# A re-tuned order for a planned macaron kernel, with a third of its last additions on two other engines

## The chip, the cores and the metric

The kernel runs on one core of a Trainium2 chip. The metric is the device time of one launch in microseconds (us), as the median over runs. The engines are named as the profile names them: PE (TensorE matmuls), DVE (VectorE), ACT (ScalarE), POOL (GpSimd) and SP (SyncE, which issues DMAs).

## The reference

The input `x` has 2 sequences of 2048 tokens with 256 features, so 4096 tokens. Three blocks follow each other, each with a residual and a layer norm in front:

```python
x = x + 0.5 * ffn(layernorm(x), gate_up, down, router)
x = x + attn(layernorm(x), conv_w, conv_b, wq, ..., proj_w, proj_b)
x = x + 0.5 * ffn(layernorm(x), gate_up, down, router)
```

`ffn` is a mixture of 8 experts of width 176. Each token goes to the 2 experts with the largest router logits, weighted by a softmax over those two; an expert computes `(silu(h @ gate) * (h @ up)) @ down`. `attn` is a causal convolution of 3 taps to queries, keys and values of width 64, then causal softmax attention with 8 heads inside blocks of 128 tokens, then two output projections. All is float32.

## The kernel before, in words

**Tiles.** The tokens lie in 8 groups of 512, each held in SBUF as `X[g]` with 4 tiles of 128 tokens. Groups 0 to 3 are one sequence, 4 to 7 the other. Each half (the first and the second `ffn`) handles the groups in two chunks: groups 0 to 2 and 3 to 7 in the first half, 0 to 4 and 5 to 7 in the second.

**A half.** For each group, `logits` normalizes the tokens, writes them to a DRAM table `hd` and computes the router logits. For each chunk, `route` (mostly small DVE steps with one-hot rows `oh` and `ot`, and PE sums `psl`) sorts the chosen tokens by expert into slots of 128 rows. `expert` then takes the slots in pairs. POOL gathers the rows of a slot from `hd` by an indirect DMA (L1113), PE transposes them into `ptr` (L1124), and DVE or ACT copies them to `hsT`. PE multiplies by gate and up into `pgu` (L1165), ACT takes a tanh (L1179), DVE finishes the gating (L1185 to L1188). PE transposes the result into `pm` (L1195), it is copied to `hmT`, PE multiplies by down into `po` (L1218, L1224), and two copies put it in `ys`. In the first half SP writes `ys` to a DRAM table `yd`. In the second half POOL scatters each slot to a table `y` (L1240). Each pair needs the register values that say which expert's weights it takes; `address` loads them for up to four slots in a row at once, for PE and for SP.

**Between the halves.** `combine` gathers the two results of each token with POOL (L1329) and adds them with DVE (L1339). `attention` normalizes again (`h_a`, L543 on DVE or L548 on ACT), runs the convolution, and then loops over 4 blocks of 128 tokens per group: scores `ps` (L1633), mask and maximum on DVE (L1642, L1651), exponentials on ACT (L1667), a product with the reciprocal of the sum on POOL (L1678), transposes `pst` (L1688), context `pcx` (L1705) and the projection with its residual (L1735).

**The end.** `gather_all` loads, for two tiles at a time, the two results of each token from `y` with SP into one of four `s` buffers (L1283, 512 KB). Four DVE additions (L1304) weight them and add them to `X[g]`, and SP stores two tiles (L1314). The loads of groups 5 to 7 need every scatter of the last chunk.

**The order of the work.** Nothing is issued in program order. Each piece is a `step` with a cost per engine that could do it, and `Plan.emit` lists the steps: the one that can start first goes next, and among those that can start at the same time, the one with the greatest priority. A step's priority is the longest chain of costs behind it plus a bias, `plan.bias`, which the table `RANK` sets for each group, chunk or stage. A step with two engines prefers the first one named and takes the other when the first is not free within 0.3 us:

```python
main = next(iter(s.costs))
if e != main and free[main] < t + 0.3:
    continue
if pick is None or t < at - 0.02 or s.prio > pick.prio:
    at, pick = t, s
```

The order found is written out and held on every engine, DMA queues of SP and POOL included. So each engine's queue is fixed, and an instruction that waits holds up all behind it on that engine. Buffers come from pools of fixed size (`SLOTS`), and a step waits for a free one.

Of the kernel before, what the change touches and what calls it, by code (L numbers as in the profile page):

```python
# [10 lines left out]
AF = mybir.ActivationFunctionType  # L11
ALU = mybir.AluOpType
# [9 lines left out]
NS = TB // P  # L22
# [35 lines left out]


RANK = {  # L60
    "logits1": (2852, 2216, 3314, 3481, 1963, 1827, 1743, 3136),
    "route1": (2091, 3734),
    "expert1": (1442, 1598),
    "fold": -360,
    "combine1": (18, 283, -268, 352, -138, -584, -694, -436),
    "attention": (31, 66, 458, -108, 359, -125, -210, -806),
    "logits2": (342, -30, -17, 461, -107, 728, -336, -232),
    "route2": (-70, 1682),
    "expert2": (-795, -757),
    "combine2": (-359, -989),  # L70
    "slope1": (168, 1),
    "slope2": (10, 184),
}


# [22 lines left out]
class Plan:  # L98
# [10 lines left out]
    def step(self, costs, fn, reads=(), writes=(), lat=None, room=(), kb=0):  # L109

        s = Step()
        s.costs, s.fn, s.lat, s.bias, s.start = costs, fn, lat, self.bias, None
        s.kb, s.land = kb, None
        deps, bufs = {}, []
        for wr, accs in ((False, reads), (True, writes)):
            for a in accs:
                b, key = a if isinstance(a, tuple) else (a, None)
                for o, k, w in b.log:  # L120
                    if (w or wr) and (k is None or key is None or k == key) and o is not s:
                        deps[id(o)] = o
                b.log.append((s, key, wr))
                if b not in bufs:
                    bufs.append(b)
                    b.left += 1
        s.used = len(bufs)
        for b in room:
            bufs.append(b)
            b.left += 1  # L130
        s.deps, s.bufs, s.outs = list(deps.values()), bufs, []
        for o in s.deps:
            o.outs.append(s)
        self.steps.append(s)
        return s
# [111 lines left out]
def kernel(  # L247
# [16 lines left out]
    nc = tc.nc  # L264
# [7 lines left out]
    plan = Plan(tc, SLOTS)  # L272
    step, buf = plan.step, plan.buf
# [12 lines left out]
    def work(tag, shape, name, dt=F32):  # L286
        return buf(pools[tag], tag, shape, name, dt)
# [26 lines left out]
    X = [fixed([P, NS, D], f"x_{g}") for g in range(NG)]  # L314
# [159 lines left out]
    for i in range(2):  # L474
        step(
            {"POOL": 0.4},
            lambda e, i=i: nc.gpsimd.iota(
                codes.t[:, i * NG * NH : (i + 1) * NG * NH], pattern=[[P, NG * NH]],
                base=(i - 1) * TOK0 + i, channel_multiplier=1,
                allow_small_or_imprecise_dtypes=True,  # L480
            ),
            writes=[(codes, i)],
# [607 lines left out]
    def expert(k, i0, n):  # L1090
        nm = f"{k.nm}_{i0}"

        beside = k.half == 2 and k.first

        def copied(act, dve):
            return {"ACT": act, "DVE": dve} if beside else {"DVE": dve, "ACT": act}
# [2 lines left out]
        for i in range(i0, i0 + n):  # L1099
# [6 lines left out]
            else:  # L1106
# [6 lines left out]
                lambda e, i=i, hs_=hs_: nc.gpsimd.indirect_dma_start(  # L1113
                    out=hs_(), out_offset=None, in_=k.h.t[:, :],
                    in_offset=bass.IndirectOffsetOnAxis(ap=k.idx.t[:, i : i + 1], axis=0),
                ),
                reads=[k.idx, k.h], writes=[(hs, m)], lat=LAND + 0.5, kb=128,
# [21 lines left out]
        for j in range(n):  # L1139
            get = step(  # L1140
                {"SP": 0.7},
                lambda e, j=j: nc.sync.dma_start(
                    wd.t[j * HALF : j * HALF + TAIL, :],
                    w_down[bass.ds(address(k, i0 + j, 1), TAIL), :],
                ),
                reads=[k.ew], writes=[(wd, j)], lat=LAND, kb=48,
# [13 lines left out]
        def gate_up(e):  # L1160
# [12 lines left out]
            reads=[hsT, k.ew] + [(wx, ("gu", c, j)) for c in range(KD) for j in range(2)],  # L1173
            writes=pgu, room=[hm],
# [5 lines left out]
            reads=[pgu[0]], writes=[hm],  # L1180
# [51 lines left out]
        for j in range(n):  # L1232
            step(
                copied(0.29, 0.34), lambda e, j=j: copy(e, ys.t[:, j, :], po[j].t),
                reads=[po[j]], writes=[(ys, j)],
# [19 lines left out]
        for to, m in [(k.y, i0)] + (  # L1255
# [8 lines left out]
                reads=[ys], writes=[(to, m + j) for j in range(n)], lat=LAND, kb=128 * n,  # L1264
# [6 lines left out]
    def gather_all(g):  # L1271

        k = chunk_of(g, 2)
        want = [(k, i) for i in range(k.NSL)]
        if k.first:
            want += [(k.next, i) for i in range(NLEFT)]
        for t in range(0, NS, 2):
            n = (g - k.g0) * NS + t
            yg = work("s", [P, 2, 2, D], f"y2_{g}_{t}")

            def get(e, t=t, yg=yg):
                r0 = 2 * (g * TB + t * P)
                ins = nc.sync.dma_start(  # L1283
                    yg.t, Y2.t[r0 : r0 + 4 * P, :].rearrange("(t p j) d -> p t j d", p=P, j=2)
                )
                apart(ins, [m for w, m in Y2.puts.items() if w not in want])
                for w in want:
                    tc.add_manual_dep(
                        ins.ins, Y2.puts[w],
                        mybir.DependencyInfo(  # L1290
                            mybir.DependencyClass.Sync, mybir.DependencyReason.DATA
                        ),
                        reason="its rows",
                    )
                Y2.gets.append(ins.ins.name)

            step(
                {"SP": 0.5}, get, reads=[(Y2, w) for w in want], writes=[yg], lat=LAND, kb=512
            )
            for i in range(2):  # L1300
                for j in range(2):
                    step(
                        {"DVE": 0.43},
                        lambda e, i=i, j=j, n=n, t=t, yg=yg: nc.vector.scalar_tensor_tensor(  # L1304
                            X[g].t[:, t + i, :], yg.t[:, i, j, :],
                            k.wt.t[:, j, n + i : n + i + 1], X[g].t[:, t + i, :],
                            ALU.mult, ALU.add,
                        ),
                        reads=[yg, k.wt], writes=[(X[g], t + i)],
                    )  # L1310
            r0 = g * TB + t * P
            step(
                {"SP": 0.35},
                lambda e, r0=r0, t=t: nc.sync.dma_start(  # L1314
                    out[r0 : r0 + 2 * P, :].rearrange("(t p) d -> p t d", p=P),
                    X[g].t[:, t : t + 2, :],
                ),
                reads=[(X[g], t), (X[g], t + 1)], lat=LAND, kb=256,
            )
# [154 lines left out]
    def attention(g):  # L1474
# [4 lines left out]
        if g % GPS == 0:  # L1479
            step(  # L1480
                {"DVE": 0.1}, lambda e: nc.vector.memset(hT.t[:, :, 0:2], 0.0),
                reads=[rstd], writes=[(hT, "pre")],
            )
        else:
# [4 lines left out]
                reads=[(lh, NH - 1), rstd], writes=[(hT, "pre")],  # L1489
# [3 lines left out]
        for i in range(NH):  # L1493
            step(
                {"POOL": 1.3},
                lambda e, i=i: nc.gpsimd.tensor_tensor(
                    X[g].t[:, 2 * i : 2 * i + 2, :], X[g].t[:, 2 * i : 2 * i + 2, :],
                    pb.t.to_broadcast([P, 2, D]), ALU.add,
                ),
                reads=[pb], writes=[(X[g], 2 * i), (X[g], 2 * i + 1)],  # L1500
# [10 lines left out]
        for n0 in (0, 3):  # L1511
# [12 lines left out]
            reads=[pqk, bias], writes=[qk],  # L1524
        )

        for i in range(2):
            step(
                {"SP": 0.52},
                lambda e, i=i: nc.sync.dma_start(kq.t[half2[i], :], qk.t[half2[1 - i], :]),  # L1530
                reads=[qk], writes=[(kq, i)], lat=LAND,
            )

        def conv_v(e):
# [13 lines left out]
            reads=[pv, bias], writes=[vb],  # L1548
        )
        vm = work("vm", [P, NS, HEADS * W], f"vm_{nm}")  # L1550
        for b0 in range(NS // 2):
# [10 lines left out]
            for i in range(2):  # L1562
                b = b0 + i * (NS // 2)
                step(
                    {"ACT": 0.49, "DVE": 0.59},
                    lambda e, b=b, p=pvm[i]: copy(e, vm.t[:, b, :], p.t),
                    reads=[pvm[i]], writes=[(vm, b)],
# [5 lines left out]
        def mmc(e):  # L1573
# [18 lines left out]
            reads=[lc, ident], writes=[pct],  # L1592
# [7 lines left out]
            reads=[pct, cb], writes=[cq],  # L1600
# [19 lines left out]
                )  # L1620

        oT = work("oT", [P, NS // 2, P], f"oT_{nm}")
        for b in range(NS):
            bs = slice(b * P, (b + 1) * P)

            s = work("s", [P, HEADS, P], f"s_{nm}_{b}")
# [113 lines left out]
    for c in range(2):  # L1740
        k = chunks[1, c]
        for g in range(k.g0, k.g1):
            plan.bias = RANK["logits1"][g]
            logits(g, 1)
            if c == 0 and g == k.g1 - 1:
                loads_then(k.rows)
        plan.bias = RANK["route1"][c]
        route(k)
        for i in range(0, k.NSL, 2):
            plan.bias = RANK["expert1"][c] - 0.1 * RANK["slope1"][c] * i  # L1750
            expert(k, i, min(2, k.NSL - i))
            if c == 0 and i == 0:
                step({"PE": 0.1}, ones_once, reads=[(k.y, 0), ones16], writes=[warm])
                plan.bias = RANK["expert1"][c] + 500.0
                hand_on(k)
                loads_last(k)
# [9 lines left out]
    for c in range(2):  # L1766
        k = chunks[2, c]
        plan.bias = RANK["route2"][c]
        route(k)
        for i in range(0, k.NSL, 2):  # L1770
            plan.bias = RANK["expert2"][c] - 0.1 * RANK["slope2"][c] * i
            expert(k, i, min(2, k.NSL - i))
            if c == 0 and i == 0:
                hand_on(k)
# [66 lines left out]
```

## Time and profile before

| what | value |
|---|---|
| median of 3 runs | 714.97 us (713.4 to 716.16) |
| the profiled execution | 717.35 us, of which the span of the profile is 715.6 |
| mean granted TensorE clock | 0.946 |
| PE busy | 650.9 us (91%) |
| DVE busy | 512.4 us (72%) |
| POOL busy | 398.6 us (56%) |
| ACT busy | 317.6 us (44%) |
| DMA | 92.59 MB, 129 GB/s on average |

All durations come from one profiled execution, which took 2.4 us more than the median. Busy time is an average over stages with different limits, so a stage is read on its own: which engine is full in it, and which wait ends last. A row of an operation gives the shortest, the median and the longest of its durations in ns. The time of one instruction contains what it waited for a shared resource after its start, so a maximum far above the median is a wait, not work.

### The profile page before, as it was taken

How to read it: one execution, taken by the hardware profiler on the slowest of the kernel's cores; microseconds unless marked ns; L12 is line 12 of the kernel's file. 1: busy time of each engine (PE TensorE's matmuls, PEld its weight loads, DVE VectorE, ACT ScalarE, POOL GpSimd, SP SyncE). 2: the span in 40 equal slices, each digit the busy share in tenths (PEclk: the TensorE clock that was granted, in tenths of full speed). 3: DMA queues.
4: the chain of work that ended last, by engine and by line, in shares of the span. 5: the costliest groups of instructions: out<-in, count | busy, mean ns of one | idle time of the engine just before them, and what ended most of it. 6: DMA issues, size and time to landing. Idle time of an engine off the chain costs nothing.

```text
span 715.6 us, 14981 instructions
## 1 busy us (share of the span) xinstructions
PE 650.9 (91%) x4837; PEld 492.9 (69%) x4837; DVE 512.4 (72%) x1408; ACT 317.6 (44%) x1008; POOL 398.6 (56%) x458
## 2 busy tenths in 40 slices
PE   6888989999999999799989997979999799999960
PEld 4647868888888754657566564657888687888840
DVE  5884984455448959998999789999845933447735
ACT  4224322222222437495997857448944233223220
POOL 4037207643337877787744622158867477777650
PEclk9699989999999999899999998979999899999995
DMA  9916616564456343023100110027224234439937
GB/s 295 305 63 188 225 49 181 181 181 142 131 139 177 123 119 88 24 59 105 38 32 30 29 47 15 17 80 231 86 87 140 65 118 131 126 110 322 323 109 264
DMA packets 64891, 92.59 MB, mean 129 GB/s; under 512 B 10128, under 2 KB 50352, under 8 KB 64720
## 3 DMA queue, kind: packets, MB, share of 16 engines
q1 hardware_dynamic: 51520, 55.31, 24.1%
q0 software_dynamic: 13296, 36.32, 17.3%
q8 instruction: 41, 0.67, 0.4%
q14 instruction: 34, 0.28, 0.1%
HBM read 56.47 MB, written 37.22 MB: 131 GB/s over the span
## 4 chain that ended last, share of the span: by engine, by line
PE 54%; DVE 33%; issue 4%; POOL 4%; DMA 4%; ACT 1%; SPq 0%; POOLq 0%; DVEq 0%; ACTq 0%
PE pgu_f L1165 20%; PE po_f L1218 8%; PE po_f L1224 5%; DVE nmx_a L1651 4%; DVE s_a L1642 4%; PE ptr_f L1124 3%; DVE x L1339 2%; PE pm_f L1195 2%; DVE oh_f L977 2%; PE pst_a L1688 2%; PE pcx_a L1705 2%; DVE stats_f L505 2%; PE pt_f L564 2%; POOL yg_f L1329 1%; DVE ot_f L985 1%
## 5 line engine op out<-in xcount | busy, mean ns | idle before, releaser
L1113 POOL DMA_INDIRECT hs_f<-hd_f,idx_f x142 | 137.1, 965 | 129.0 <-PE ptr_f L1124 40.6
L1165 PE MATMUL pgu_f<-wx,hsT_f 128*128 x1136 | 184.0, 318 | 1.8 <-DVE hsT_f L299 0.8
L1165 PEld LDWEIGHTS pgu_f<-wx,hsT_f 128*128 128x128 f32 x1136 | 172.7, 193 | 7.5 <-issue 2.6
L1667 ACT ACTIVATE s_a<-s_a,nmx_a 128x128 f32<-128x128 f32 x256 | 98.9, 392 | 11.8 <-DVE nmx_a L1653 11.2
L1678 POOL TENSOR_TENSOR s_a<-s_a,sm_a 128x512 f32<-128x512 f32 x64 | 67.0, 1069 | 61.4 <-DVE sm_a L1674 59.7
L1240 POOL DMA_INDIRECT y<-ys_f,dst_f x71 | 71.0, 1000 | 33.5 <-ACT ys_f L295 13.9
L295 ACT COPY ys_f<-po_f 128x256 f32<-128x256 f32 x123 | 40.8, 375 | 109.8 <-PE po_f L1224 92.4
L1179 ACT ACTIVATE hm_f<-pgu_f 128x352 f32<-128x352 f32 (+1 forms) x72 | 33.0, 460 | 108.8 <-PE pgu_f L1165 106.5
L1218 PE MATMUL po_f<-wx,hmT_f 128*128 x284 | 76.6, 392 | 0.7 <-DVE hmT_f L299 0.7
L1185 DVE SCALAR_TENSOR_TENSOR hm_f<-hm_f,pgu_f 128x352 f32<-128x352 f32 (+1 forms) x72 | 36.7, 510 | 56.2 <-ACT hm_f L1179 55.9
L1329 POOL DMA_INDIRECT yg_f<-yd_f,posi_f x64 | 61.7, 964 | 24.9 <-issue 15.3
L1218 PEld LDWEIGHTS po_f<-wx,hmT_f 128*128 128x128 f32 x284 | 49.5, 192 | 10.6 <-DVE hm_f L1188 3.3
L299 DVE COPY hmT_f<-pm_f 128x384 f32<-128x384 f32 x40 | 22.2, 556 | 44.1 <-PE pm_f L1196 43.9
L1224 PE MATMUL po_f<-wd_f,hmT_f 48*128 48x256 f32 x284 | 51.1, 432 | 0.0
L1339 DVE SCALAR_TENSOR_TENSOR x<-yg_f,wt_f,x 128x256 f32<-128x256 f32 x64 | 41.6, 674 | 11.0 <-DMA yg_f<-yd_f,posi_f 11.0
L1667 ACT ACTIVATION_READ_ACCUMULATOR s_a<-s_a,nmx_a 128x1 f32 x256 | 49.0, 192 | 0.0
L1515 PE MATMUL pqk_a<-haT_a,cw 128*128 128x512 f32 x96 | 46.3, 630 | 0.5 <-ACT haT_a L295 0.5
L1124 PE MATMUL ptr_f<-ident,hs_f 128*128 128x128 f32 x284 | 42.2, 276 | 2.4 <-DMA hs_f<-hd_f,idx_f 2.4
L1688 PE MATMUL pst_a<-ident,s_a 128*128 128x128 f32 x256 | 37.1, 287 | 4.5 <-DVE vm_a L299 2.9
L1642 DVE TENSOR_TENSOR s_a<-ps_a,later 128x512 f32<-128x512 f32 x64 | 40.5, 678 | 0.0
L1688 PEld LDWEIGHTS pst_a<-ident,s_a 128*128 128x128 f32 x256 | 29.2, 146 | 16.3 <-issue 9.5
L1651 DVE TENSOR_REDUCE nmx_a<-s_a 128x8 f32<-128x1024 f32 x32 | 38.7, 1210 | 0.2
(235 smaller groups left out, 1228.0 us busy)
## 6 DMA issues: line engine op xcount, KB each, us to landing
yd_f<-ys_f SPq DMA_DIRECT2D x42, 256.0 KB, 3.6
hd_f<-h_f SPq DMA_DIRECT2D x32, 256.0 KB, 3.2
y<-y SPq DMA_DIRECT2D x16, 512.0 KB, 5.3
wd_f<-in_w_down SPq DMA_DIRECT2D x142, 48.0 KB, 2.7
x<-in_x SPq DMA_DIRECT2D x16, 256.0 KB, 7.0
out<-x SPq DMA_DIRECT2D x16, 256.0 KB, 3.2
hd_f<-hd_f SPq DMA_DIRECT2D x1, 2560.0 KB
hs_f<-hd_f,idx_f POOLq DMA_INDIRECT x142
```

The lines of the kernel that those rows point to most:

```text
L1113: lambda e, i=i, hs_=hs_: nc.gpsimd.indirect_dma_start(out=hs_(), out_offset=None, in_=k.h.t[:, :], in_offset=bass.IndirectOffsetOnAxis(ap ...
L1124: nc.tensor.transpose(pt.t[:, d, j, :], hs_()[:, d * P : (d + 1) * P], ident.t)
L1165: nc.tensor.matmul(pgu[f].t[:, j, :], hsT.t[:, d, j, :], wx.t[:, bass.ds(at + d * GU + f * H, H)], start=(d == 0), stop=(d == KD - 1),)
L1218: nc.tensor.matmul(po[j].t, hmT.t[:, j, :], wx.t[:, bass.ds(at + KD * GU, D)], start=True, stop=False,)
L1224: nc.tensor.matmul(po[j].t, hmT.t[r, n, :], wd.t[r, :], start=False, stop=True)
L1240: ins = nc.gpsimd.indirect_dma_start(out=Y2.t[:, :], out_offset=bass.IndirectOffsetOnAxis(ap=k.dst.t[:, i : i + 1], axis=0), in_=ys.t[:, j ...
L1329: lambda e, j=j, n=n, yg=yg: nc.gpsimd.indirect_dma_start(out=yg.t, out_offset=None, in_=k.y.t[:, :], in_offset=bass.IndirectOffsetOnAxis( ...
L1642: lambda e, h=hd[i], s=s, p=ps[i]: nc.vector.tensor_tensor(s.t[:, h, :], p.t, later.t.to_broadcast([P, NPAIR, P]), ALU.add,),
L1651: nc.vector.tensor_reduce(nmx.t, s.t, AX.X, ALU.max)
L1667: nc.scalar.activation(s.t[:, n, :], s.t[:, n, :], AF.Exp, bias=nmx.t[:, n : n + 1], accum_out=sm.t[:, c : c + 1],)
L1678: lambda e, s=s, sm=sm, h=hd[i]: nc.gpsimd.tensor_tensor(s.t[:, h, :], s.t[:, h, :], sm.t.unsqueeze(2).to_broadcast([P, NPAIR, P]), ALU.mu ...
L1688: nc.tensor.transpose(pt.t[:, c, :], s.t[:, i * NPAIR + c, :], ident.t)
```

## The change

Four things change.

1. The table `RANK` has new values throughout, and new entries: a bias for each pair of slots in each of the four expert stages (`pairs10`, `pairs11`, `pairs20`, `pairs21`, by half and chunk) and one for each of the 32 blocks of attention (`blocks`).
2. In the first chunk of both halves the copies of `expert` name ACT first. Before, that held for the first chunk of the second half only.
3. In `gather_all`, every third tile of the last chunk (4 of the 12 tiles in groups 5 to 7) is scaled in place by ACT and added by POOL; the other tiles keep DVE's additions. A DVE addition now depends on its own tile's part of the loaded buffer.
4. The planner's cost of a last addition on DVE is 0.41 instead of 0.43.

```diff
 RANK = {
-    "attention": (31, 66, 458, -108, 359, -125, -210, -806),
+    "attention": (432, 467, 901, -42, 551, -142, -313, -806),
...
+    "pairs10": (-72, 245, 231, -387, -412, -403, -649, 1, -735),
+    "pairs11": (0, 6, 6, 4, -114, -114, -113, -117, -116, -115, ...),
+    "pairs20": (0, -1, 0, 5, 23, -9, 3, 1, -3, -7, -4, 0, -1, 1, 3, -2, 0),
+    "pairs21": (39, 317, -36, 78, -166, -81, -144, -416, -215, ...),
+    "blocks": (4, 4, 5, 4, 4, 4, 4, 4, 4, 4, ..., 54, -26, -8),
 }
...
-        beside = k.half == 2 and k.first
+        beside = k.first
...
             for i in range(2):
+                if not k.first and (NS * (g - k.g0) + t + i) % 3 == 2:
+
+                    def scaled(e, i=i, n=n, yg=yg):
+                        for j in range(2):
+                            nc.scalar.activation(
+                                yg.t[:, i, j, :], yg.t[:, i, j, :], AF.Copy,
+                                scale=k.wt.t[:, j, n + i : n + i + 1],
+                            )
+
+                    step({"ACT": 0.62}, scaled, reads=[k.wt], writes=[(yg, i)])
+
+                    def added(e, i=i, t=t, yg=yg):
+                        for j in range(2):
+                            nc.gpsimd.tensor_tensor(
+                                X[g].t[:, t + i, :], X[g].t[:, t + i, :], yg.t[:, i, j, :],
+                                ALU.add,
+                            )
+
+                    step({"POOL": 1.1}, added, reads=[(yg, i)], writes=[(X[g], t + i)])
+                    continue
                 for j in range(2):
                     step(
-                        {"DVE": 0.43},
+                        {"DVE": 0.41},
...
-                        reads=[yg, k.wt], writes=[(X[g], t + i)],
+                        reads=[(yg, i), k.wt], writes=[(X[g], t + i)],
...
+        bias0 = plan.bias
         for b in range(NS):
+            plan.bias = bias0 + RANK["blocks"][NS * g + b]
...
-            plan.bias = RANK["expert1"][c] - 0.1 * RANK["slope1"][c] * i
+            plan.bias = (
+                RANK["expert1"][c] - 0.1 * RANK["slope1"][c] * i
+                + RANK["pairs1" + str(c)][i // 2]
+            )
```

The same addition is made to the bias of the second half's pairs.

## The prediction

> **What bounds the kernel now.** I read the page first (engine totals, the 40 slices), then busy time by stretch, then the chain and the timeline of the end, and last the rows of the operations that the change moves. Busy time of each engine in seven stretches (columns: stretch, its length, then PE, PE weight loads, DVE, ACT, POOL, granted clock, DMA share, GB/s):
>
> ```profile
> 62.00:100.00 38.00, 34.48 (x230) 29.29 (x229) 31.46 (x99) 12.55 (x30) 10.84 (x13) 0.87 0.51 159
> 100.00:235.00 135.00, 134.70 (x877) 114.36 (x875) 74.55 (x172) 33.47 (x88) 68.04 (x73) 1.00 0.53 153
> 235.00:300.00 65.00, 60.19 (x392) 35.94 (x388) 56.53 (x127) 30.94 (x100) 51.19 (x55) 0.95 0.32 94
> 300.00:400.00 100.00, 94.54 (x857) 63.19 (x853) 96.85 (x248) 79.84 (x304) 61.19 (x68) 0.98 0.17 49
> 400.00:472.00 72.00, 63.50 (x572) 41.30 (x571) 61.96 (x182) 42.41 (x151) 24.73 (x29) 0.92 0.10 27
> 472.00:693.00 221.00, 214.63 (x1512) 177.75 (x1512) 137.99 (x376) 96.58 (x292) 157.67 (x166) 0.97 0.48 154
> 693.00:716.00 23.00, 0.00 (x0) 0.00 (x0) 10.01 (x25) 0.36 (x1) 2.75 (x3) 0.57 0.65 228
> ```
>
> Four regimes follow. From 100 to 235 (experts of the first half) PE is busy 134.7 of 135.0: nothing but less PE work helps there. From 300 to 400 (attention) DVE has 96.85 of 100 and PE 94.54, so DVE work added or removed there counts nearly in full. From 472 to 693 (experts of the second half) PE is the bound again, with 6.4 us idle. After 693 PE has nothing left, and 23 us are the last scatters, loads, additions and stores. This is the timeline of that end (start, duration, engine, line, operation, count, idle before):
>
> ```profile
> 690.29 0.97 POOL L1240 DMA_INDIRECT y<-ys_f,dst_f  x1 [0.30 <-issue]
> 691.11 1.13 PE L1218 MATMUL po_f<-wx,hmT_f 128*128 x4 [0.65 <-DVE hmT_f L299]
> 695.39 0.97 POOL L1240 DMA_INDIRECT y<-ys_f,dst_f  x1 [0.30 <-issue]
> 698.04 5.67 SPq L1283 DMA_DIRECT2D y<-y  x5
> 701.65 8.01 DVE L1304 SCALAR_TENSOR_TENSOR x<-y,wt_f,x 128x256 f32<-128x256 f32 x20 [8.32 <-DMA y<-y]
> 704.93 0.36 SPq L1283 DMA_DIRECT2D y<-y  x1
> 710.25 1.67 DVE L1304 SCALAR_TENSOR_TENSOR x<-y,wt_f,x 128x256 f32<-128x256 f32 x4 [0.59 <-DMA y<-y]
> ```
>
> The scatters are spaced 1.27 us on POOL and run 2.5 us past PE's end. The first loads land at 701.65. The sixth load is issued only at 704.93, when the eighth addition has given back one of the four `s` buffers. It lands 5.3 us later, and four additions and a store end the program. So DVE's additions count twice: through the buffer they free (until 704.93), and as the last four after 710.25. Between the two DVE even waits 0.59. The rows of the operations that are moved, or compete with those moved (ns minimum/median/maximum), and a stretch of timeline that shows how:
>
> ```profile
> L1339 DVE SCALAR_TENSOR_TENSOR x<-yg_f,wt_f,x x64: 447/478/3148, 213.5 to 385.2; 128x256 f32<-128x256 f32 x64
> L1304 DVE SCALAR_TENSOR_TENSOR x<-y,wt_f,x x64: 470/479/507, 648.0 to 711.4; 128x256 f32<-128x256 f32 x64
> L548 ACT ACTIVATE h_a<-x,shift_a,rstd_a x18: 584/598/612, 232.9 to 411.9; 128x256 f32<-128x256 f32 x18
> L543 DVE TENSOR_SCALAR h_a<-x,mv_a,rstd_a x14: 398/407/4312, 233.1 to 415.4; 128x256 f32<-128x256 f32 x14
> 283.56 4.64 DVE L543 TENSOR_SCALAR h_a<-x,mv_a,rstd_a 128x256 f32<-128x256 f32 x2
> 283.69 4.02 POOL L1678 TENSOR_TENSOR s_a<-s_a,sm_a 128x512 f32<-128x512 f32 x4
> 289.72 0.62 PE L1688 MATMUL pst_a<-ident,s_a 128*128 128x128 f32 x3 [2.86 <-DVE vm_a L299]
> ```
>
> The same addition takes 478 to 479 ns at the median in both uses, but at most 507 at the end of the program, where POOL only issues DMAs, and up to 3148 beside POOL's arithmetic. At 283.56 a `h_a` step of DVE (two instructions, 0.72 us at another place) stood 4.64 us, while POOL ran four products without a gap; PE then waited 2.86 us for what was queued behind it.
>
> **The change part by part.** Every count below is from comparing the order of the built instructions of the two programs; every duration is from a row of before. Each sum is against the profiled execution, 717.35 us (span 715.6 and 1.75 around it). That one is 2.4 us above the median of the runs, 714.97, to which the difference is then applied.
>
> *First chunk's copies, ACT first.* Up to the first expert pair the two orders differ only in which group is normalized first. DVE loses the first pair's `hsT` copy (0.61 us, here 0.58 on ACT) and four later copies. From 62 to 100 DVE is the bound (31.46 of 38, and PE waits for its one-hot rows), but the copy ran at 60.51, next to waits of DVE of 2.4 and 1.6 us, and ACT has to do it on the same path. I take -0.2 (0 to -0.6). The cover is that DVE idles there; without it the gain is one copy.
>
> *Pairs in another order.* Each pair costs the same matmuls. In both orders the first-half gathers all stand ahead of the first `combine` gather on POOL, and `combine` waits for all of `y`. In the PE-bound stretch the distance from a pair's gate/up matmuls to its transposes is at least some 2.9 us of other PE work in the new order, against about 1.4 us that the ACT and DVE steps between them take. So 0. Out of order the index loads no longer serve four slots each: 44 instead of 38 on PE and on SP. Before shows no PE gap at any of the 38, so 0.2 (0 to 1.2, at 0.2 each, the smallest gap I listed).
>
> *Priorities in attention.* Block order changes inside groups 0, 3, 4 and 7. By counts, DVE takes three more `h_a` steps (14 to 20 instructions; groups 5 and 6) and gives two `vm`, one `u`, two `oT` and one `hT` copy to ACT. The row of DVE's `h_a` between 230 and 400 has 12 at 8.3 us busy, so 0.69 each with their waits for POOL: +4.1. What leaves is 2 x 0.60 + 0.66 + 2 x 0.25 + 0.60 = -3.0. ACT is relieved of six `h_a` and takes the copies. DVE is full there, so +1.1 (between -3, if relieving ACT, 79.84 of 100, takes waits out, and +5, rival two).
>
> *End of the expert stage.* After the last gate/up matmuls PE now has two down-projections, two transposes, two down-projections, where it had two, one, one. The 0.65 us for `hmT` falls to some 0.2, because a second pair's transposes lie between. I count that at nothing: the cover is POOL's queue of scatters, which runs 2.5 us past PE's end and never waits in it. What counts is that queue, now eight long instead of six. From the end of the gate/up the old last scatter starts after 8.8 us; the new one after 2.4 + 7 x 1.27 = 11.3, but 2.25 us of PE work (a down-projection 1.7, transposes 0.55) has moved behind that mark. So +0.3 (-0.5 to +1).
>
> *A third of the last additions.* Only four of the twelve tiles of the last three groups move: 8 of the last 24 additions become 8 ACT scalings and 8 POOL additions; the 40 of the first five groups stay. Loads now come as 5b, 6a, 7a, 7b (each with one moved tile), then 5a and 6b on SP behind them, the latter behind a store as before. The fifth and sixth loads take the buffers of 5b and 6a. These come free after two scalings (two instructions of the ACT row above took 1.08), then two POOL additions. Before has no 128x256 addition on POOL; its 128x512 rows take 1.03 and 1.27. Proportional would be 0.52 to 0.64, all fixed cost 1.27; I take 0.6, since I expect size to count. Then 5b is free at 701.65 + 1.1 + 0.1 + 1.2 = 704.05, and 6a 1.2 later, 705.25, against 704.93. Add 0.3 for waits between DVE and POOL: +0.6 (-0.2 to +2.8). Behind the waiting store and the sixth load on SP stand only stores, and on ACT and POOL nothing follows the new work. The last load's four additions are still DVE's, so the stretch after it stays 1.67.
>
> Here a rule speaks against the change. The timeline at 283.56 shows DVE stopped while POOL computes. The Trainium skill, page "SBUF — State Buffer", section "Who interferes with whom", calls the port pair that DVE and GpSimd share an exclusive lock, so moving work between those two does not make it parallel. By it the last three groups need 16 x 0.40 + 8 x 0.6 = 11.2 us of one port, against 24 x 0.40 = 9.6: +1.6. By the rows it is +0.6, since in those 10.3 us the loads, not the port, set the last step. I use the row, and keep 1.6 in the range.
>
> Sum: -0.2 + 0.2 + 1.1 + 0.3 + 0.6 = +2.0; profiled 719.4, median 714.97 + 2.0 = 717.0. A difference of 0.5%, 3.6 us, is about the least that a measurement of this kernel tells from none, so 2.0 is forecast as no difference.
>
> **The rivals.**
> - *The priorities take stalls out (faster).* PE is idle 5.5 us in 300 to 400 and 6.4 in 472 to 693, and the clock is granted at less than full there (0.98 and 0.97 on average, 2 and 6.6 us). If half of the idle time and a third of that clock loss go, that is 5.9 + 2.9 = 8.8 less; with 0.9 of the sum that stays, -7.9: 707, or with two thirds of it, 710. For it: ACT is relieved where it is busiest. Against: the long waits, for `ot`, `mask` and `vm`, stand at places whose order on DVE is unchanged.
> - *The port decides (slower).* If one of the three new `h_a` steps starts against a train of four POOL products, as at 283.56, DVE stands 4.6 - 0.7 = 3.9 us more where it is full, and PE's wait brings a slower clock (0.89 in 270 to 300, 3 us there). One such train gives 2.0 + 3.9 = 5.9: 720.9; with the clock 724. It decides from 1.6 us on DVE, since with the sum that passes 718.5. For it: group 5's `h_a` now stand among group 4's products. Against: the median of such steps is clean, 407 ns.
> - *It does not do what it says.* Equal pairs swapped, equal work: 715 within 1. This belongs to no difference.
>
> **How the numbers follow.** No difference (711.4 to 718.5) 0.43, its own range 713.5 to 718.4; stalls gone 0.22; the port, with the dearest POOL additions and index loads, 0.35. Leaving a tenth at each end gives 709 to 724.
>
> **What would show it.** Right: PE full from 100 to 235; last scatter 3 us after PE's end; sixth load issued 0.3 us or so later in its stretch; additions of DVE at the end over 507 ns where POOL adds. Wrong on the gain side: PE idle in 300 to 472 well under 14 us. On the loss side: a `h_a` on DVE of groups 5 or 6 above 2 us. POOL additions of over 1 us would sink the last part, and a wait of PE at an index load the second.

## The result, and the profile after

The changed kernel takes 722.44 us (median of 6 runs, 718.58 to 724.23), the kernel before 715.58 (6 runs, 713.4 to 716.42). The ratio is 1.0081, with a 95% interval of 1.0055 to 1.0107: 5.8 us slower (3.9 to 7.7; the two medians lie 6.9 apart), where 717.0 within 709 to 724 was forecast, as no difference.

The two profiled executions lie unluckily. That of the kernel before, 717.35 us, is slower than the median; that of the changed kernel, 718.58, is the fastest of its six, at a granted clock of 0.955 where the other five had 0.939 to 0.951. So the two traces differ by 1.2 us where the medians differ by 6.9, and a trace can show where time is lost, not all of it. The same seven stretches as before, now of the changed kernel:

```profile
62.00:100.00 38.00, 34.35 (x242) 28.51 (x240) 33.34 (x102) 12.26 (x29) 9.89 (x12) 0.91 0.49 151
100.00:235.00 135.00, 134.68 (x875) 114.14 (x873) 71.48 (x168) 38.33 (x95) 71.55 (x76) 1.00 0.53 156
235.00:300.00 65.00, 60.19 (x411) 36.43 (x409) 56.22 (x129) 32.00 (x103) 49.92 (x56) 0.95 0.31 88
300.00:400.00 100.00, 94.70 (x861) 63.00 (x857) 96.80 (x252) 82.94 (x327) 64.19 (x70) 1.00 0.18 50
400.00:472.00 72.00, 61.96 (x546) 41.14 (x547) 62.67 (x184) 37.23 (x124) 22.58 (x28) 0.93 0.10 27
472.00:693.00 221.00, 212.76 (x1494) 174.37 (x1490) 140.49 (x375) 92.55 (x282) 156.02 (x162) 0.98 0.47 152
693.00:716.00 23.00, 0.00 (x0) 0.00 (x0) 9.74 (x17) 3.79 (x9) 9.83 (x12) 0.58 0.69 228
```

The first five rows are those of before to within 1.6 us of PE's busy time. The row that changes is the sixth, the experts of the second half: PE is idle 8.2 us instead of 6.4, although PE is the bound there. One wait of 2.65 us is more than that difference. The timeline of the changed kernel around it (start, duration, engine, line, operation, count, idle before and its releaser):

```profile
641.53 7.17 SPq L1288 DMA_DIRECT2D y<-y  x5
...
642.24 0.46 ACT L1184 ACTIVATE hm_f<-pgu_f 128x352 f32<-128x352 f32 x1 [2.25 <-DVE hm_f L1193]
...
645.48 0.67 PE L1223 MATMUL po_f<-wx,hmT_f 128*128 x2
...
646.65 1.67 DVE L1329 SCALAR_TENSOR_TENSOR x<-y,wt_f,x 128x256 f32<-128x256 f32 x4 [4.44 <-DMA y<-y]
...
648.24 0.51 DVE L1190 SCALAR_TENSOR_TENSOR hm_f<-hm_f,pgu_f 128x352 f32<-128x352 f32 x1
...
648.80 1.09 PE L1223 MATMUL po_f<-wx,hmT_f 128*128 x2 [2.65 <-DVE hm_f L1190]
```

The tanh of a pair is done at 642.7, and DVE could begin its gating (L1190). But the first four of the last additions (L1329, the first two tiles of group 0) stand ahead of the gating on DVE's queue. Their load was issued at 641.53 and lands at 646.65, so DVE stands still for 4.44 us, and the gating starts at 648.24. The profile names that gating as the releaser of PE's next matmuls: PE waits 2.65 us in the middle of the stretch where it is the bound. These matmuls are the second half of an earlier pair's down-projection, and in the code they read nothing that the gating writes. What can link them is a PSUM bank: `bank` is a pool of eight, and L1190 is the last to read the first `pgu` bank of the gated pair. That is read from the code; no run tests it.

Here the clock follows. Busy time of each engine and the granted clock (columns as in the table above) in the changed kernel, before, during and after that wait:

```profile
640.00:646.00 6.00, 6.00 (x41) 4.99 (x39) 1.69 (x4) 2.10 (x6) 4.47 (x6) 1.00 0.62 145
646.00:649.00 3.00, 0.35 (x2) 0.20 (x2) 2.25 (x6) 0.38 (x1) 2.39 (x3) 1.00 1.03 401
649.00:652.00 3.00, 3.00 (x9) 1.71 (x9) 2.97 (x9) 0.37 (x1) 2.39 (x3) 0.50 1.04 382
```

After 2.65 us without work PE gets half its clock for 3.4 us (649.0 to 652.4, in finer stretches), and does 9 matmuls in 3 us, where e1 below does 19 to 23 at full clock. That costs another 1.7 us, an estimate: half of 3.4.

The end of the changed kernel, to be laid beside the timeline of before:

```profile
698.69 6.81 SPq L1288 DMA_DIRECT2D y<-y  x5
702.66 0.91 ACT L1310 ACTIVATE y<-y,wt_f 128x256 f32<-128x256 f32 x2 [9.50 <-DMA y<-y]
...
703.26 7.05 POOL L1319 TENSOR_TENSOR x<-x,y 128x256 f32<-128x256 f32 x8 [6.26 <-ACT y L1310]
...
704.02 4.84 DVE L1329 SCALAR_TENSOR_TENSOR x<-y,wt_f,x 128x256 f32<-128x256 f32 x6 [0.35 <-DMA y<-y]
...
706.88 0.36 SPq L1288 DMA_DIRECT2D y<-y  x1
...
711.84 1.67 DVE L1329 SCALAR_TENSOR_TENSOR x<-y,wt_f,x 128x256 f32<-128x256 f32 x4 [0.45 <-DMA y<-y]
```

From the first landing to the last addition it takes 10.85 us (702.66 to 713.51) against 10.27 before, although DVE has 16 additions instead of 24. Six of them took 4.84 us, 0.81 each, while POOL was adding too.

### The profile page after: what moved, and what is told of

It reads as the page before. It is cut to its first block, busy times and chain, and to the rows that moved or that the text cites. A ratio compares the mean times of both kernels' runs of the same rounds, so it can differ in the third digit from the quotient of the medians.

```text
span 716.9 us, 15024 instructions
## 1 busy us (share of the span) xinstructions
PE 648.0 (90%) x4837; PEld 489.9 (68%) x4837; DVE 513.3 (72%) x1405; ACT 322.0 (45%) x1011; POOL 407.2 (57%) x466
## 4 chain that ended last, share of the span: by engine, by line
PE 58%; DVE 30%; DMA 4%; issue 3%; POOL 2%; ACT 2%; SPq 0%; DVEq 0%; POOLq 0%; ACTq 0%
PE pgu_f L1170 21%; PE po_f L1223 8%; PE po_f L1229 6%; PE ptr_f L1129 4%; DVE s_a L1669 4%; DVE nmx_a L1678 3%; PE pm_f L1200 2%; DVE oh_f L982 2%; PE pcx_a L1732 2%; PE pst_a L1715 2%; DMA y<-y 2%; DVE stats_f L510 2%; PE pt_f L569 2%; PE ps_a L1660 2%; DVE x L1364 2%
## 5 line engine op out<-in xcount | busy, mean ns | idle before, releaser
L300 ACT COPY ys_f<-po_f 128x256 f32<-128x256 f32 x114 | 38.2, 375 | 111.7 <-PE po_f L1229 102.2
L1190 DVE SCALAR_TENSOR_TENSOR hm_f<-hm_f,pgu_f 128x352 f32<-128x352 f32 (+1 forms) x72 | 36.7, 510 | 46.0 <-ACT hm_f L1184 45.9
L525 POOL TENSOR_TENSOR rstd_f<-rstd_f,mhalf 128x4 f32<-128x4 f32 x16 | 17.5, 1094 | 38.7 <-DVE jmp_f L881 19.4
```

## The experiments

Each of these kernels was timed in five rounds beside the kernel before on the same chip; the row of the change is the result above. e1 to e4 ran on a chip where the kernel before takes 715.71 us, e5 to e8 on a second one where it takes 802.98, and e9 to e13 on a third where it takes 802.54, so all times are read as ratios to the kernel before on the same chip; intervals are 95%. Theory S says that the wait at the first additions is the loss, theory T that the moved last additions are, theory A that attention's new order is.

| kernel | ratio | interval |
|---|---|---|
| the change | 1.0081 | 1.0055 to 1.0107 |
| e1: the change, first additions behind the gating | 1.0028 | 1.0017 to 1.004 |
| e2: before, first additions ahead of the gating | 1.0056 | 1.0037 to 1.0075 |
| e3: the change, last additions back on DVE | 1.009 | 1.0063 to 1.0117 |
| e4: before, last additions of four tiles moved | 1.0053 | 1.0034 to 1.0072 |
| e5, e13: e1 and e3 together, two times | 1.0004, 1.0008 | 0.9982 to 1.0027, 0.997 to 1.0047 |
| e6, e12: before, ACT first in the first chunk, two times | 1.0011, 0.9998 | 0.9983 to 1.0039, 0.9975 to 1.0021 |
| e7: before, moved tiles 0, 3, 6, 9 | 1.002 | 0.9999 to 1.0041 |
| e8: before, four tiles scaled by ACT, added by DVE | 0.9988 | 0.9963 to 1.0013 |
| e9: before, spare buffers for the last loads | 1.0 | 0.9977 to 1.0023 |
| e11: e9 and tiles 0, 2, 4 moved | 0.9967 | 0.9944 to 0.999 |

**e1 and e2, the wait alone, taken away and put in.** In e1 four instructions of the changed kernel change places on DVE:

```diff
-x<-y_0_0 (four additions)
 hm_f_1_14 gating (L1190 to L1193)
+x<-y_0_0 (four additions)
```

> The changed kernel with one move: DVE's four additions of the first two tiles (x<-y_0_0) go behind the next gating step instead of ahead of it; every other order is as in the changed kernel. Theory S (the stall): DVE stands 4.4 us at these additions for their load, the gating behind them comes late, PE waits 2.65 us and then has 3.4 us at half clock, so some 4 of the 6.9 us come from here: about 718.5 us, ratio to the kernel before 1.004, and the PE wait near 646 us is gone. Theory T (the last additions) and theory A (attention's order): unchanged, 722.4 us, ratio 1.0095.

It takes 717.73 us (22 runs): with one move 4.7 us of the 6.9 between the medians are gone (by the ratios 3.8 of 5.8, give or take 2), as theory S says. DVE still waits for the load, as the timeline of e1 shows, but with nothing behind it that PE needs:

```profile
644.32 0.52 DVE L1200 SCALAR_TENSOR_TENSOR hm_f<-hm_f,pgu_f 128x352 f32<-128x352 f32 x1 [0.53 <-ACT hm_f L1194]
...
648.16 3.32 DVE L1339 SCALAR_TENSOR_TENSOR x<-y,wt_f,x 128x256 f32<-128x256 f32 x8 [2.47 <-DMA y<-y]
```

Busy time and granted clock of e1 in the stretches that answer to those above:

```profile
641.00:647.00 6.00, 6.00 (x43) 5.27 (x41) 2.92 (x7) 1.97 (x6) 4.74 (x5) 1.00 0.58 142
647.00:650.00 3.00, 3.00 (x19) 2.25 (x17) 1.84 (x5) 1.34 (x3) 2.13 (x3) 1.00 1.03 373
650.00:653.00 3.00, 3.00 (x23) 2.99 (x22) 2.98 (x8) 0.47 (x1) 2.39 (x3) 1.00 1.04 391
```

PE has no gap and keeps its full clock.

In e2 the same four additions of the kernel before go ahead of the gating that stood before them; one scatter of POOL moved behind two gathers with it.

```diff
+x<-y_0_0 (four additions)
 hm_f_1_18 gating
 ys_f_1_16 copy
-x<-y_0_0 (four additions)
```

> The kernel before with the opposite move: the same four additions go ahead of the gating step that stood before them. Theory S: the load lands at 648.0 and the gating is then done at 650.9, where PE wants it at 648.0, so PE waits some 3 us and the clock may drop for 3.4 us: 718.5 to 720.5 us, ratio 1.004 to 1.007. Theories T and A, by which such a wait is taken up by the scatters and loads that follow: within 1 us of the kernel before.

720.14 us, 4.4 us slower than the kernel before. Its timeline has the same three steps, additions that wait, gating behind them, PE behind that:

```profile
647.97 1.72 DVE L1314 SCALAR_TENSOR_TENSOR x<-y,wt_f,x 128x256 f32<-128x256 f32 x4 [2.86 <-DMA y<-y]
...
649.62 0.51 DVE L1195 SCALAR_TENSOR_TENSOR hm_f<-hm_f,pgu_f 128x352 f32<-128x352 f32 x1
...
651.05 0.41 PE L1205 MATMUL pm_f<-ident,hm_f 128*128 128x128 f32 x2 [2.13 <-DVE hm_f L1198]
```

The wait is therefore shown from both sides: without it the loss shrinks, and with it the kernel before gets slower. Its size is less sure. In e2's trace PE waits 2.13 us, and the clock behind that wait stays full:

```profile
648.00:651.00 3.00, 0.92 (x7) 0.65 (x5) 2.93 (x8) 0.46 (x1) 2.32 (x3) 1.00 1.03 375
651.00:654.00 3.00, 2.95 (x20) 2.97 (x21) 2.86 (x8) 0.94 (x2) 2.39 (x3) 1.00 1.04 313
```

So that trace shows some 2.2 us of e2's 4.4, and where the others go is open. In e3, which keeps the changed kernel's order on DVE, the wait is there again (4.07 us of DVE, 2.28 of PE), and behind it the clock is halved again:

```profile
649.35 1.67 DVE L1326 SCALAR_TENSOR_TENSOR x<-y,wt_f,x 128x256 f32<-128x256 f32 x4 [4.07 <-DMA y<-y]
...
651.51 1.08 PE L1223 MATMUL po_f<-wx,hmT_f 128*128 x2 [2.28 <-DVE hm_f L1190]
```

```profile
652.00:654.00 2.00, 2.00 (x7) 0.84 (x6) 2.00 (x6) 0.19 (x1) 1.39 (x3) 0.50 1.05 391
```

The half clock thus followed two of the three waits, and is no fixed part of their price.

Why the planner puts the additions first can be read in its code, but no run tests it. It gives a load's issue 0.5 us and lets it land `LAND` = 2.3 us later, or for 512 KB at `RATE` = 240 at least 2.1 + 1.0 = 3.1 us later, so 3.6 us from the start of the issue. From there the load took 5.1 us in the changed kernel and 4.6 in the kernel before. With the gating at about the same planned time as the landing, a change of priorities may put the additions first.

**e3 and e4, the last additions alone.** In e3 the steps of ACT are emptied and those of POOL issue DVE's additions, at the same place of the order:

```diff
-nc.scalar.activation(yg[i, j], yg[i, j], AF.Copy, scale=k.wt[j, n + i])
-nc.gpsimd.tensor_tensor(X[g][t + i], X[g][t + i], yg[i, j], ALU.add)
+nc.vector.scalar_tensor_tensor(X[g][t + i], yg[i, j], k.wt[j, n + i], X[g][t + i], ALU.mult, ALU.add)
```

In e4 the kernel before gets the two engines' work, one scaling and one addition where each of DVE's additions stood:

```diff
+if not k.first and (NS * (g - k.g0) + t + i) % 3 == 2:
+    nc.scalar.activation(yg[i, j], yg[i, j], AF.Copy, scale=k.wt[j, n + i])
+    nc.gpsimd.tensor_tensor(X[g][t + i], X[g][t + i], yg[i, j], ALU.add)
```

> The changed kernel with the sixteen instructions of the last additions that ACT and POOL have given back to DVE (eight additions in place of eight scalings and eight additions), at the same place of the order; all else as in the changed kernel. Theory T: the scalings and POOL's additions hold the buffers longer and collide with DVE's, so taking them away gives 1.5 us or more: 721 or less, ratio 1.0075 or less. Theory S and A: within 1 us of 722.4; and if the two engines do help, slower by up to 1 us, 723.4.

> The kernel before with only the last additions of the same four tiles (every third of the last chunk) on ACT and POOL, in the same place of the order. Theory T: slower by 1 to 2 us, 717 us, ratio 1.002 or so, as the port between DVE and POOL takes 1.6 us more and the sixth load is issued later. Rival (the engines work beside each other): DVE has 3.4 us less in a stretch in which it was busy for 8.0 us, the sixth load goes 0.5 to 1.5 us earlier: 714 to 715, ratio 0.998 to 1.

e3 takes 721.92 us: in the changed kernel no difference can be told by which engine those additions run on. Its interval (1.0063 to 1.0117) just reaches the 1.0075 that T asked, so a gain of 1.5 us is not excluded by the times alone; but the end of the program is only 0.5 us shorter in its trace (20.3 against 20.8, table below). Theory T falls as the main cause of the loss. But e4 takes 719.24 us, 3.5 us more than the kernel before, about twice what T asked. The difference is the order of the loads. In the changed kernel the four loads with moved tiles come first; in e4 the last load holds moved tile 11, and its additions on POOL are the last work of all. From the last scatter to the end e4 takes 23.4 us where the kernel before takes 20.25, and the row of the end of the program shows what sets it. The closing DRAIN of each engine's queue, in e4:

```profile
L1851 POOLq DRAIN  x3: 45/107/6158, 710.6 to 717.3; - x3
L1851 SPq DRAIN  x3: 7/7/7, 713.8 to 717.0; - x3
```

and in the kernel before:

```profile
L1837 POOLq DRAIN  x3: 45/176/7867, 693.9 to 715.4; - x3
L1837 SPq DRAIN  x3: 7/7/7, 714.4 to 715.0; - x3
```

SP's drain of e4, behind the last store, is over at 713.9, and the program could end as the kernel before does. But POOL's drain runs until 716.73, which is 5.4 us after POOL's last addition ended (711.33), and the program ends 0.8 us later. POOL's last additions in e4:

```profile
709.61 1.72 POOL L1309 TENSOR_TENSOR x<-x,y 128x256 f32<-128x256 f32 x2 [1.03 <-ACT y L1305]
```

The distance is the same wherever POOL stops: in the kernel before the drain ends at 701.74, 5.4 us after the last scatter's issue ended (696.36), and nothing waits for it. In the changed kernel it ends at 715.71, 0.4 us ahead of SP's last drain: that cost is just hidden.

**e7 and e8, which part of the moved additions it is.** e7 is e4 with other tiles, so that the last load has no moved tile; e8 is e4 with DVE's addition for POOL's.

```diff
 e7
-(NS * (g - k.g0) + t + i) % 3 == 2
+(NS * (g - k.g0) + t + i) % 3 == 0
 e8
-nc.gpsimd.tensor_tensor(X[g][t + i], X[g][t + i], yg[i, j], ALU.add)
+nc.vector.tensor_tensor(X[g][t + i], X[g][t + i], yg[i, j], ALU.add)
```

> The kernel before with four moved tiles as in the kernel with only the last additions moved, but tiles 0, 3, 6 and 9 instead of 2, 5, 8 and 11, so that none lies in the last load. Theory D (POOL's closing drain, which ended 5.4 us after POOL's last addition in three traces, sets the end): POOL's last addition ends some 2.7 us earlier, its drain is then over before the last store has landed, and the 3.5 us shrink to 1 or less: 716 to 716.7 us, ratio 1.001. Theory P (DVE and POOL hold each other up, or POOL's additions are too slow): the work is the same, so still 3 us or more: 718.7, ratio 1.004 or more.

> The kernel before with the same four tiles scaled by ACT, but added by DVE, so that POOL does no arithmetic at the end. Theory D: without POOL's arithmetic the drain is over early, and DVE's work is as before; 715.5 to 716.5 us, ratio 1.0005. Theory of the ACT step (the extra hand-over between engines costs the 3.5 us): 718 or more, ratio 1.0035.

The intervals are wide on the slower chips. e8 (0.9988, at most 1.0013) rules out the hand-over to ACT as the cost. e7 (1.002) cannot tell the two theories apart by its time; its trace can. Its end, from the last scatter, takes 21.4 us, 0.65 more than the 20.75 of e8 and e12 on those chips, instead of 3.15 more, and POOL's drain, over at 801.34 with the last addition at 795.94, again ends 5.4 us behind it and still 0.5 us behind SP's. So the drain is the larger part of e4's longer end of 3.15 us: by the two drains of e4's trace it is 2.8 us (716.73 against 713.9), and some 2.5 at the program's end, which comes 0.8 us after POOL's drain in e4 and 1.15 after SP's in the kernel before.

**e5 and e6, the rest.** e5 (and e13, the same again) joins e1 and e3; e6 (and e12) is the kernel before with one line of the change:

```diff
-beside = k.half == 2 and k.first
+beside = k.first
```

> Both edits together on the changed kernel: the first four additions behind the gating, and the last additions of the moved tiles back on DVE. What is left of the change is the new priorities, ACT first and the new order of the last loads. If the parts add up (stall 4.4 us, moved last additions 0.3 us at this place): 717.5 us, ratio 1.0025. If the moved additions had hidden behind the stall, they show now: 716.5 or less, ratio 1.001. If they help, 719, ratio 1.0045.

> The changed kernel with the first four additions behind the gating and the last additions back on DVE, a second time, for the same reason. If the parts add up (stall 4.4 us, moved last additions 0.3 us): ratio 1.0025. If the new priorities and the longer queue of scatters cost nothing: 1.0005 or less.

> The kernel before with only the second part of the change, ACT first for the copies of the first chunk in the first half (five copies go from DVE to ACT; one pair's gate/up comes earlier on PE). By the prediction's sum: 0 to 0.6 us faster, ratio 0.9992 to 1. Rival: ACT now holds the first pair's copy behind a logits copy, and the first gate/up waits for it (0.93 us in the trace of the changed kernel): 0.9 us slower, ratio 1.0013.

> The kernel before with only ACT first in the first chunk, a second time, as the first interval of 0.9983 to 1.0039 was too wide. By the prediction's sum 0 to 0.6 us faster, ratio 0.9992 to 1; rival: the first gate/up waits for ACT, 0.9 us slower, ratio 1.0013.

What is left of the change in e5, all new priorities and the new order at the end of PE, cannot be told from the kernel before (1.0004 and 1.0008), nor can ACT first (1.0011 and 0.9998). The spread on these chips, 0.2% to 0.4% either way, does not tell 0.6 us from 2.

**e9 and e11, a try for a better end.** In the kernel before the sixth load waits for a buffer. In e9 the last two loads use two buffers of attention's `vm`, free by then; in e11 three tiles are moved too, all in the first three loads.

```diff
-yg = work("s", [P, 2, 2, D], f"y2_{g}_{t}")
+yg = work("vm" if (g, t) in ((7, 0), (7, 2)) else "s", [P, 2, 2, D], f"y2_{g}_{t}")
```

> The kernel before, where the last two loads of y (x<-y_7_0 and y_7_2) use two buffers of attention that are free by then, so that no load waits for an addition; on SP one store moves behind the last load, nothing else changes. Theory B (the sixth load's wait for a buffer sets the end): the last load lands at about 708 instead of 710.2, and the end comes 2 us earlier: 713.6 us, ratio 0.997. Theory V (DVE is then the bound: 24 additions of 0.42 us from 701.65 on end at 711.7): 0.2 to 0.4 us earlier, ratio 0.9995.

> As the kernel with spare buffers, and three tiles of the last chunk (0, 2 and 4, all in the first three loads) scaled by ACT and added by POOL. Theory V: DVE has 18 additions, so the last load's landing at about 708.1 sets the end: additions until 709.8, last store landed at 712.4, end at 713.3 against 715.6 in the span, 2.3 us faster than the kernel before, 713.3 us, ratio 0.997. Theory D puts a floor under it: POOL's last addition at about 706.8, its drain until 712.2. Theory P (DVE and POOL hold each other up): no faster than the kernel with spare buffers alone.

The end of e9:

```profile
780.23 3.00 SPq L1284 DMA_DIRECT2D y<-y  x6
784.00 9.59 DVE L1305 SCALAR_TENSOR_TENSOR x<-y,wt_f,x 128x256 f32<-128x256 f32 x24 [9.89 <-DMA y<-y]
```

and of e11:

```profile
778.71 3.00 SPq L1284 DMA_DIRECT2D y<-y  x6
...
782.50 1.00 DVE L1319 SCALAR_TENSOR_TENSOR x<-y,wt_f,x 128x256 f32<-128x256 f32 x2 [9.91 <-DMA y<-y]
783.09 5.32 POOL L1310 TENSOR_TENSOR x<-x,y 128x256 f32<-128x256 f32 x6 [6.07 <-ACT y L1306]
...
783.84 8.81 DVE L1319 SCALAR_TENSOR_TENSOR x<-y,wt_f,x 128x256 f32<-128x256 f32 x16 [0.33 <-DMA y<-y]
```

In e9 no load waits, and DVE is the bound as theory V says: 24 additions without a gap, 0.40 us apart. In e11 DVE has only 18 and yet needs 10.15 us (782.50 to 792.65) instead of 9.59: of DVE's six additions that begin while POOL adds, five last 0.77 to 0.94 us, and those after POOL is done 0.47. The shorter end by which theory V forecast 2.3 us did not come, and theory P is right on this point: six additions moved to POOL cost DVE more than their own time. From the last scatter to the end e9 takes 19.7 us and e11 20.0, against 20.75 in e8 and e12. By its ratio e11 is the fastest kernel (0.9967, at most 0.999), and the ratio is the very one that theory V asked (0.997). But its end accounts for 0.8 of the 2.6 us only, and e9, whose end is shorter still by 0.2 us, measures no gain. So e11 beats the kernel before by its interval, which overlaps that of e9 and is the one of a dozen that ends just below 1, so chance is not excluded. Its moved tiles are not shown to be the reason, and where the rest comes from is open.

## Why the prediction was right or wrong

The time, 722.44, lies in the range. The likeliest case, no difference at 717.0, did not come; slower did, which had 0.35. The time even lies where the rival of the port put it, 720.9 to 724, but the mechanism that made it slower is none of the three cases. That the range held is luck.

The step that failed is "Pairs in another order", "So 0". It compared the 2.9 us between a pair's gate/up and its transposes with the 1.4 us of ACT's and DVE's own work, and did not ask what else stands between them on DVE's queue. There stood four additions and a wait of 4.4 us for a load. The two orders on DVE's queue show the additions in front, and the timeline of before showed the wait, 1.91 us ahead of the same additions at 648, with a gating in front:

```profile
643.39 2.14 SPq L1283 DMA_DIRECT2D y<-y  x4
...
644.32 0.51 DVE L1185 SCALAR_TENSOR_TENSOR hm_f<-hm_f,pgu_f 128x352 f32<-128x352 f32 x1
...
647.99 1.67 DVE L1304 SCALAR_TENSOR_TENSOR x<-y,wt_f,x 128x256 f32<-128x256 f32 x4 [1.91 <-DMA y<-y]
```

Nor were the pair's own transposes what waited first, but the down-projection of an earlier pair. Left out was a term that e1 measures at 4.7 us by the medians. The trace of the changed kernel shows 2.65 us of PE's wait for it and about 1.7 of the half clock behind it; from the last `psl` to PE's end e1 is 3.0 us shorter (125.0 against 128.0, table below), so not all of that sum is gained.

Without that term the prediction's sum of +2.0 is met: e1 is 2.0 us slower than the kernel before (1.2 to 2.9). That is luck too. The parts as the traces show them below (0, 0, -0.8, +0.4, about 0, +0.6) add to +0.2, not 2.0, e1's profiled span is 0.6 us shorter than that of the kernel before, and where e1 loses the 2.0 us is not shown.

The other steps can be laid against the traces by stage. The table divides the span at three points: the end of the last routing sums (`psl`), PE's end and the start of the last scatter. e4 and e2 have the order of before up to the point where they were changed, e1 and e3 that of the change.

| us | to the last `psl` | to PE's end | to the last scatter | to the end |
|---|---|---|---|---|
| before | 567.4 | 125.5 | 2.5 | 20.25 |
| e2 | 568.2 | 127.8 | 2.5 | 20.4 |
| e4 | 565.5 | 126.2 | 2.5 | 23.4 |
| the change | 564.7 | 128.0 | 3.4 | 20.8 |
| e1 | 566.1 | 125.0 | 3.4 | 20.5 |
| e3 | 568.1 | 127.3 | 3.4 | 20.3 |

- First copies, -0.2: not seen. The first gate/up starts at 60.0 to 63.3 in both orders, by how long PE waited for the first gather (0.3 to 2.4 us). Where the gather is early, PE then waits for ACT (0.93 us in the changed kernel), so ACT is late next. e6 and e12 see no difference.
- Index loads, +0.2: no PE gap above 0.3 us at any of them, so nothing.
- First-half pairs, 0: from the first to the last gate/up 177.0, 177.4 and 177.6 us with the new order, 178.2, 178.2 and 178.0 with the old: 0.8 better, in three traces each.
- Attention, +1.1: from there to the last `psl` 327.1 to 327.6 us against 326.6 to 327.5, some +0.4, with ranges that overlap. The longest of the six new `h_a` instructions took 1.12 us, so the rival of the port did not happen where it was placed; the three new steps took 3.1 us instead of 4.1. PE idles 15.3 us from 300 to 472 (14.0 before), so the faster rival did not happen either. No run has attention's priorities alone.
- End of PE, +0.3: the last scatter comes 3.4 us behind PE's end instead of 2.5, as forecast (3), and PE's end comes earlier for it: from the last `psl` to the last scatter e1 takes 128.4, the kernel before and e4 128.0 and 128.7. The wait for `hmT` fell from 0.65 to 0.32.
- Last additions, +0.6: measured 0.58 from the first landing to the last addition. The parts were off and cancelled: the sixth load goes out 4.2 us after the first landing (3.3 before, 3.6 forecast), since POOL's addition has a median of 0.84 us, not 0.6, although ACT's two scalings took 0.91, not 1.08. DVE's last additions then begin 4.96 us after that load's issue, where they began 5.32 after it before.

The last step also bears on the weighing of that rule on the port of DVE and POOL. These are the rows of the changed kernel:

```profile
L1329 DVE SCALAR_TENSOR_TENSOR x<-y,wt_f,x x56: 471/478/943, 646.6 to 713.0; 128x256 f32<-128x256 f32 x56
L1319 POOL TENSOR_TENSOR x<-x,y x8: 784/843/998, 703.3 to 709.5; 128x256 f32<-128x256 f32 x8
```

The maximum of the additions at the end was 507 ns before; it is 943 now. The rule (of the Trainium skill, "SBUF — State Buffer", "Who interferes with whom": DVE and GpSimd take the pair in turn) gave +1.6 for the changed kernel, the rows +0.6. The price in the changed kernel is the smaller one, for the reason named, since the loads set the last step there. In e11, where the loads do not, the rule is right in direction: what went to POOL came back as waiting on DVE. Added up strictly it asks too much. POOL's last addition in e4, with DVE done, took 0.72 us (710.61 to 711.33), so 18 x 0.40 + 6 x 0.72 would give some 11.5 us (an estimate); without any sharing it is 7.2; e11 needs 10.15.

## What to carry to other kernels

Before an order is judged, look for each instruction on the critical path at what stands directly ahead of it on its engine, and whether that waits for a transfer: here four cheap additions cost some 4 to 5 us because one gating step was queued behind their load. If a planner writes the order, compare its assumed landing times with the trace (3.6 us assumed, 4.6 to 5.1 measured for this load) before searching over its priorities. If POOL computes near the end of a program, look at when its closing DRAIN ends: arithmetic of POOL that ended last cost most of e4's loss, and in the changed kernel, where it ended earlier, nothing that e3 can tell. Do not count an addition given to POOL as one that DVE is relieved of: with six of them on POOL, DVE's last additions took 0.6 us longer, not shorter (e11 against e9).

## What the runs showed of the hardware that was not expected

- POOL's closing DRAIN ended 5.4 us after POOL's last instruction in all the traces read for it, whether that was an addition (e4, e7, e11, the change) or a scatter's issue (before, e3). In these traces it set the end only where POOL's last work ended late: in e4 and e7 it was over 2.8 and 0.5 us after SP's last wait, in the changed kernel 0.4 us before.
- An addition of DVE (128x256) lasts 0.47 to 0.48 us alone, with one begun every 0.40 (e9), and mostly 0.77 to 0.94 beside additions of POOL (e11, the change).
- A PE wait of 2.65 us (the change) was followed by 3.4 us at half the granted clock, and so was one of 2.28 us (e3), but one of 2.13 us (e2) was not. Where it came, it added more than half of the wait again.
- Two other chips run the kernel before in 803 us instead of 716. There PE stood still for 7.3 to 9.5 us at the same places in e6, e9 and e12 (near 65 and near 297 us), with ACT or DVE waiting for something that the profile calls remote. The cause was not looked for.
